# Attention output multiplied straight from PSUM, and four neighbours reordered, in a one-core decoder layer

## The chip, the cores and the metric

The kernel runs on one core of one Trainium2 chip. The metric is the device time of one execution in microseconds (us); a time is the median of several executions. The engines of the core are named as in the profile: PE (TensorE, matrix products and transposes), DVE (VectorE), ACT (ScalarE), POOL (GpSimd) and SP (SyncE, which issues nearly all DMAs here). Every engine works through its own list of instructions in order, and instructions on different engines wait for each other through semaphores.

## The reference, cut to what matters

One decoder layer on 32 batch elements of 256 tokens and 256 features, in float32: self attention with 16 heads of 64 (4 key and value heads, rotary positions, ALiBi bias), windowed cross attention with 16 heads of 16, and a feed-forward net with quantized weights and activations. Each part is followed by a residual and a layernorm.

```python
# self attention, the part that the change touches
q, k, v = x @ Wq, x @ Wk, x @ Wv          # 16 heads of 64; k and v of 4 heads
attn = q @ k.T / 8 + slopes * (key position - query position)
attn = softmax(attn)                      # over 256 keys
out  = (attn @ v) @ Wo
x = layernorm(x + out)
x = layernorm(x + cross_attention(x, ctx, cell))
x = layernorm(x + feed_forward(x))
```

## The kernel before, in words

**Tiling.** Tokens come in two tiles of 128 (`NT`), features in two chunks of 128 (`NDC`). Self attention of a batch element is cut into eight units (`self_units`, L383): two query tiles x two pairs of key heads x two halves of the heads that share them. A *pair* `m` is two units that share query tile and key heads; there are four pairs per batch element and 128 in all. Cross attention has four units per batch element.

**One self unit.** `self_scores` (L385) multiplies queries and keys into two PSUM banks `s`; DVE adds the ALiBi row and takes the minimum for the softmax in one instruction (L409). `self_exp` (L421) takes the exponential on ACT and sums it (L427). `self_turn` (L460) transposes the exponentials on PE into a bank `t` (L470) and ACT copies it out as `pT` (L475).

**One pair.** `self_values` (L477) multiplies `v` with four `pT` tiles into one bank `o` (L487); ACT copies the bank into the SBUF tile `oT` (L494). The softmax sums are turned separately: `self_inverse` (L436) takes the reciprocal on DVE (L441), DVE spreads it into the tile `wide` (L443), a transposing DMA on SP moves `wide` to `planes` (L448), and `self_spread` (L452) interleaves `planes` into `R` on POOL (L455). `wide`, `planes` and `R` have one buffer each. `self_normal` (L496) then multiplies `oT` by `R` on DVE (L500).

**Other work, cut into parts.** The projections (`self_inputs`, L330 to L354), the output projection and first layernorm (`self_output`, L502 to L555: the product `wo` L508, the factors `rs_x` on POOL L523 to L526, the normalized row `zq` on DVE L533, its transpose `zqT` copied out by ACT as `zT` L205, and the product `xq` L545), the cross attention's input (`cross_inputs`, with the factors `rstd_zc` L184 to L186 and the scaling of `cs` on ACT L198), its output and the feed-forward net (`feed_forward`: the products `ff` L811, tanh on ACT L825 and the products on DVE L826, the rounding steps L798 on POOL and L800 on DVE) are generators. At each `yield` a generator gives the number of slots until its next part.

**Order.** A loop written out by hand runs over slots, four to a pair (L905 to L953). In each slot it emits fixed steps of self attention and cross attention, and `parts()`, which emits the parts that are due. `flush()` at a slot's end emits what the parts have put off, such as the scaling of `cs`. For PE, DVE and ACT the order of emission is the order of execution (`manual_schedule`, L895). For POOL and SP a scheduler places the instructions, so a change in the emission order can move instructions on these two queues that the diff does not name. In slot 0 the two score units, four groups of exponentials, the values of pair `m - 1` and the cross attention's transposes come first; in slot 1 the parts, the cross attention's scores, values and half of its exponentials; in slot 2 the parts, the reciprocals and the transposes of the first unit; in slot 3 the transposes of the second unit, the parts and the spreading.

**Banks.** All PE outputs share one pool of eight PSUM banks (`bank`, L91). A bank that is read by ACT or DVE is free for a new product when that read has ended.

Of the kernel before, what the change touches and what calls it, by code (L numbers as in the profile page):

```python
# [14 lines left out]
ALU = mybir.AluOpType  # L15
# [36 lines left out]
def kernel(  # L52
# [27 lines left out]
    nc = tc.nc  # L80
# [5 lines left out]
    def ctile(shape, dtype, name):  # L86
        return const.tile(shape, dtype, name=name, tag=name)
# [3 lines left out]
    def bank(name, shape=(P, 512), dtype=F32):  # L91
        return ps.tile(list(shape), dtype, tag="b", name=name)
# [10 lines left out]
    def work(name, shape, bufs=2, dtype=F32):  # L103
        return sb.tile(list(shape), dtype, tag=name, name=name, bufs=bufs)
# [50 lines left out]
    for i in range(2):  # L155


        t = ctile([P, (NT + 1) * XH * XE + 32 - XE], F32, f"xvaug{i}")
# [33 lines left out]
    def flush():  # L192
        while last:
            last.pop(0)()
# [282 lines left out]
    def self_values(b, m):  # L477

        s = state[b]
        qc, kc, _rp = self_units[2 * m]  # L480
        pTs = [s.pop(("pT", 2 * m + rp)) for rp in range(2)]
        s["oT", qc, kc] = oT = work("oT", [P, NCH // 2, P], 3)
        po = bank("o")
        for kk in range(NT):
            for rp in range(2):
                for half in range(2):
                    nc.tensor.matmul(  # L487
                        po[half * HD : (half + 1) * HD, rp * L : (rp + 1) * L],
                        s["v"][:, kk, (2 * kc + half) * HD : (2 * kc + half + 1) * HD],
                        pTs[rp][half][:, kk * L : (kk + 1) * L],  # L490
                        start=(kk == 0 and rp == 0),
                        stop=(kk == NT - 1 and rp == 1),
                    )
        nc.scalar.copy(oT.rearrange("p c t -> p (c t)"), po)  # L494

    def self_normal(b, m):  # L496
        s = state[b]
        qc, kc, _rp = self_units[2 * m]
        oT = s["oT", qc, kc].rearrange("p c t -> p (c t)")
        nc.vector.tensor_tensor(oT, oT, s.pop(("R", m)), ALU.mult)  # L500

    def self_output(b, qc):  # L502

# [391 lines left out]
    with tc.manual_schedule(engines={mybir.EngineType.PE, mybir.EngineType.DVE, mybir.EngineType.Activation}):  # L895
        running = []
        slot = min(starts)
        while starts or running:
            m, part = divmod(slot, 4)
            k = m - CROSS  # L900
            for gen in starts.pop(slot, ()):
                running.append([slot, gen])

            def cross(f, unit, *more):
                if 0 <= unit < 4 * B:  # L905
                    f(*divmod(unit, 4), *more)

            def pair(f, unit):
                if 0 <= unit < 4 * B:
                    f(*divmod(unit, 4))  # L910

            def own(f, unit, *more):
                if 0 <= unit < 8 * B:
                    f(*divmod(unit, 8), *more)

            def parts():
                for r in list(running):
                    if r[0] == slot:
                        wait = next(r[1], r)
                        if wait is r:  # L920
                            running.remove(r)
                        else:
                            r[0] += wait or 1

            if part == 0:
                own(self_scores, 2 * m)
                own(self_scores, 2 * m + 1)
                own(self_exp, 2 * m, 0)
                own(self_exp, 2 * m, 1)
                own(self_exp, 2 * m + 1, 0)  # L930
                pair(self_values, m - 1)
                cross(cross_turn, k - 1, 0)
                cross(cross_turn, k - 1, 1)
                own(self_exp, 2 * m + 1, 1)
                parts()
                pair(self_normal, m - 1)
            elif part == 1:
                parts()
                cross(cross_scores, k)
                cross(cross_values, k - 1)  # L940
                cross(cross_exp, k, 0)
            elif part == 2:
                parts()
                pair(self_inverse, m)
                cross(cross_exp, k, 1)
                own(self_turn, 2 * m)
                cross(cross_back, k - 1)
            else:
                own(self_turn, 2 * m + 1)
                parts()  # L950
                pair(self_spread, m)
            flush()
            slot += 1  # L953
# [89 lines left out]
```

## Time and profile before

| what | us |
|---|---|
| median of 3 executions | 2209.63 (2208.27 to 2213.26) |
| the profiled execution, whole | 2211.08 |
| its span, first to last instruction | 2209.3 |
| PE busy | 2103.3 (95%) |
| DVE busy | 1789.9 (81%) |
| ACT busy | 1659.5 (75%) |
| POOL busy | 1316.8 (60%) |
| L494, ACT copy of `o` into `oT`, 128 times | 72.0 (563 ns each) |
| L500, DVE product `oT` x `R`, 128 times | 98.0 (765 ns each) |
| L455, POOL copy into `R`, 128 times | 173.5 (1356 ns each) |
| L443, DVE spreading of the reciprocals, 128 times | 108.2 (845 ns each) |

The busy times overlap, so they do not add up to the span. A group's idle time is the time that its engine stood still just before it, and its releaser is the instruction whose end let it go on. A timeline row gives the start and duration in us, the engine, the line, the operation, what it writes and reads, and in brackets the idle time before it with its releaser.

### The profile page before, as it was taken

The numbers are of one execution on the slowest core, as the hardware profiler recorded it, in microseconds if no ns is written. First come the engines' busy times: TensorE is split into PE (matmuls) and PEld (weight loads), VectorE is DVE, ScalarE is ACT, GpSimd is POOL, SyncE is SP. The second block draws the span as 40 slices with busy tenths as digits, with TensorE's granted clock in tenths as the row PEclk, the third lists the DMA queues.
The fourth block names the chain that finished last, engine by engine and source line by source line (L and its number), as shares of the span: only waits on it lengthen the run. The fifth ranks groups of instructions, "written<-read, shape, count | busy, mean of one in ns | idle before, by whom it ended". The sixth has DMA issues, their size and how long they took to land.

```text
span 2209.3 us, 54605 instructions
## 1 busy us (share of the span) xinstructions
PE 2103.3 (95%) x17254; PEld 1617.7 (73%) x17316; DVE 1789.9 (81%) x6949; ACT 1659.5 (75%) x4961; POOL 1316.8 (60%) x1977
## 2 busy tenths in 40 slices
PE   7899999999999999999999999999999999999984
PEld 5677777777777777777777777777777777777662
DVE  3877888888888888888888888888888888888775
ACT  2578778787778787778777778877777877777862
POOL 4465655666665666655656655656666556666542
PEclk8999999999999999999999999999999999999985
DMA  6433333333333334333333333334333333333221
GB/s 213 113 78 71 82 78 76 75 78 85 84 79 73 79 74 86 88 76 75 78 74 90 83 75 74 80 74 89 84 79 77 78 73 83 85 78 74 43 52 31
DMA packets 326592, 177.59 MB, mean 80 GB/s; under 512 B 242976, under 2 KB 296096, under 8 KB 326304
## 3 DMA queue, kind: packets, MB, share of 16 engines
q1 hardware_dynamic: 324608, 170.52, 34.1%
q10 hardware_dynamic: 1696, 3.57, 0.4%
q8 instruction: 138, 2.26, 0.4%
q14 instruction: 150, 1.23, 0.2%
HBM read 39.50 MB, written 8.39 MB: 22 GB/s over the span
## 4 chain that ended last, share of the span: by engine, by line
PE 58%; DVE 20%; ACT 12%; DMA 3%; issue 2%; POOL 1%; SPq 0%; ACTq 0%; POOLq 0%; DVEq 0%
PE wo L508 9%; PE t L470 8%; DVE p L409 7%; PE s L393 6%; ACT p L427 6%; PE o L487 5%; PE proj L330 5%; PE ff L811 4%; PE xq L545 3%; PE xt L708 3%; ACT xpT L710 3%; PE ffo L858 3%; PE xk L617 2%; PE xw L770 2%; PE v L362 2%; DMA out_dram<-x 2%
## 5 line engine op out<-in xcount | busy, mean ns | idle before, releaser
L427 ACT ACTIVATE p<-p,nm 128x256 f32<-128x256 f32 x1024 | 508.3, 499 | 235.8 <-DVE nm L409 235.8
L409 DVE CUSTOM_DVE_ANT_0 p<-s,alibi 128x256 f32<-128x256 f32 x1024 | 361.6, 416 | 3.2 <-PE s L393 3.2
L699 ACT ACTIVATE xp<-xp,xnm 128x128 f32<-128x128 f32 x1024 | 328.6, 401 | 47.0 <-DVE xnm L683 46.8
L393 PE MATMUL s<-kT,qT 64*128 64x256 f32 x2048 | 271.4, 392 | 0.0
L475 ACT COPY pT<-t 128x512 f32<-128x512 f32 x512 | 263.7, 598 | 7.0 <-PE t L470 6.8
L470 PE MATMUL t<-ident,p 128*128 128x128 f32 x2048 | 267.0, 273 | 0.9 <-ACT p L427 0.9
L354 POOL TENSOR_TENSOR qT<-qT,other 128x512 f32<-128x512 f32 x128 | 178.7, 1396 | 137.9 <-DMA other<-psin 113.1
L487 PE MATMUL o<-pT,v 128*64 128x256 f32 x2048 | 249.8, 386 | 0.0
L393 PEld LDWEIGHTS s<-kT,qT 64*128 64x128 f32 x2048 | 197.5, 187 | 68.6 <-issue 16.2
L330 PE MATMUL proj<-xT,wq_sb 128*128 128x256 f32 x1024 | 245.8, 384 | 0.0
L508 PE MATMUL wo<-wo_sb,oT 128*128 128x256 f32 x1024 | 244.1, 381 | 0.4 <-DVE oT L500 0.4
L470 PEld LDWEIGHTS t<-ident,p 128*128 128x128 f32 x2048 | 234.9, 142 | 9.4 <-ACT p L427 2.6
L683 DVE CUSTOM_DVE_ANT_0 xp<-xs,mask 128x128 f32<-128x128 f32 x1024 | 225.5, 284 | 13.2 <-PE xs L669 11.0
L508 PEld LDWEIGHTS wo<-wo_sb,oT 128*128 128x128 f32 x1024 | 192.9, 191 | 29.3 <-DVE oT L500 1.1
L487 PEld LDWEIGHTS o<-pT,v 128*64 128x64 f32 x2048 | 136.4, 137 | 98.1 <-issue 42.3
L330 PEld LDWEIGHTS proj<-xT,wq_sb 128*128 128x128 f32 x1024 | 187.7, 193 | 21.9 <-issue 0.4
L500 DVE TENSOR_TENSOR oT<-oT,R 128x512 f32<-128x512 f32 x128 | 98.0, 765 | 119.8 <-ACT oT L494 110.2
L427 ACT ACTIVATION_READ_ACCUMULATOR p<-p,nm 128x1 f32 x1024 | 194.1, 190 | 0.0
L455 POOL COPY R<-planes 128x1024 uint16<-128x1024 uint16 x128 | 173.5, 1356 | 21.9 <-DMA planes<-wide 21.6
L826 DVE SCALAR_TENSOR_TENSOR gu<-gu,ff 128x512 f32<-128x512 f32 x128 | 82.5, 684 | 100.7 <-ACT gu L825 100.6
L847 POOL TENSOR_SCALAR gu<-gu,ffhup 128x1024 f32<-128x1024 f32 x64 | 73.5, 1149 | 143.9 <-DVE ffhup L843 143.9
L708 PEld LDWEIGHTS xt<-ident,xp 128*128 128x128 f32 x1024 | 112.1, 143 | 49.0 <-issue 36.2
(147 smaller groups left out, 4530.8 us busy)
## 6 DMA issues: line engine op xcount, KB each, us to landing
other<-psin SPq DMA_DIRECT2D x640, 64.0 KB, 2.0
xT<-in_xt_dram SPq DMA_DIRECT2D x32, 256.0 KB, 2.8
xs<-in_x_dram SPq DMA_DIRECT2D x32, 256.0 KB, 2.7
cs<-in_ctx_dram SPq DMA_DIRECT2D x32, 256.0 KB, 2.8
other<-qb SPq DMA_DIRECT2D x64, 128.0 KB, 2.0
kTz<-tr SPq DMA_DIRECT2D x256, 32.0 KB, 2.0
other<-qb SPq DMA_DIRECT2D x128, 64.0 KB, 1.9
out_dram<-x SPq DMA_DIRECT2D x32, 256.0 KB, 2.4
```

Of the source, the lines that this page charges most:

```text
L330: nc.tensor.matmul(pq[:, c * L : (c + 1) * L], w[:, dc, c * P : (c + 1) * P], xT[:, dc, :], start=(dc == 0), stop=(dc == NDC - 1),)
L354: nc.gpsimd.tensor_tensor(d2, d2, other, ALU.add)
L393: nc.tensor.matmul(banks[half][:, rr * L : (rr + 1) * L], qT[rows_, rr, qc * P : (qc + 1) * P], kT[rows_, kc, :], start=(rr == 0), stop=(r ...
L409: nc.vector.tensor_tensor_reduce(p[:, cols], banks[half][:, cols], alibi[:, 2 * (4 * kc + 2 * rp + rr) + half, :], -0.125, 3.0e38, ALU.add ...
L427: nc.scalar.activation(p[:, cols], p[:, cols], AF.Exp, bias=nm[:, rr : rr + 1], scale=-1.0, accum_out=s["sums", i // 2][:, e : e + 1],)
L470: nc.tensor.transpose(pt[:, j * P : (j + 1) * P], p[half][:, rr * L + kk * P : rr * L + (kk + 1) * P], ident,)
L475: nc.scalar.copy(pT[half], pt)
L487: nc.tensor.matmul(po[half * HD : (half + 1) * HD, rp * L : (rp + 1) * L], s["v"][:, kk, (2 * kc + half) * HD : (2 * kc + half + 1) * HD], ...
L508: nc.tensor.matmul(py[:, 0:D], s["oT", qc, kc][:, r, :], wo_sb[:, 4 * kc + r, :], start=(kc == 0 and r == 0), stop=(kc == 1 and r == 3),)
L683: nc.vector.tensor_tensor_reduce(p[:, cols], banks[2 * half + j // 2][:, j % 2 * P : (j % 2 + 1) * P], s["mask"][:, qc, :], -1.0, 3.0e38, ...
L699: nc.scalar.activation(p[:, cols], p[:, cols], AF.Exp, bias=s["xnm", i][half][:, j : j + 1], scale=-1.0)
L708: nc.tensor.transpose(pt[:, j * P : (j + 1) * P], p[:, j * P : (j + 1) * P], ident)
```

## The change

The ACT copy of `o` into `oT` is taken out: `self_values` keeps the bank, and `self_normal` reads the bank on DVE and writes `oT`. In slot 0 `parts()` is emitted ahead of the last group of exponentials instead of behind it. In slot 2 `self_inverse` is emitted ahead of `parts()`. In slot 3 `parts()` is emitted ahead of the transposes of the second unit.

```diff
@@ self_values
-        nc.scalar.copy(oT.rearrange("p c t -> p (c t)"), po)
+        s["po", m] = po
@@ self_normal
-        nc.vector.tensor_tensor(oT, oT, s.pop(("R", m)), ALU.mult)
+        nc.vector.tensor_tensor(oT, s.pop(("po", m)), s.pop(("R", m)), ALU.mult)
@@ slot 0
                 cross(cross_turn, k - 1, 1)
+                parts()
                 own(self_exp, 2 * m + 1, 1)
-                parts()
                 pair(self_normal, m - 1)
@@ slot 2
+                pair(self_inverse, m)
                 parts()
-                pair(self_inverse, m)
                 cross(cross_exp, k, 1)
@@ slot 3
+                parts()
                 own(self_turn, 2 * m + 1)
-                parts()
                 pair(self_spread, m)
```

On POOL and SP the changed program stands in another order too. On SP the transposing DMA of `planes` moves forward. On POOL the copy into `R` (L455), which stood behind `rs_x` (L523 to L526) twice per batch element, stands ahead of it; once it stands ahead of `rstd_zc` (L184 to L186) and once ahead of L579 to L581. The first of the three products of the rotary step, L579, stands ahead of L798, where it stood behind.

## The prediction

> **What bounds the kernel now.** I read the table of stretches first, then the waits of TensorE (PE), then the timelines of all engines over one round. Between 70 us and 2140 us, at a granted clock of 1.00, PE is busy 2017.25 of 2070.00 us, and one wait holds most of the rest.
>
> ```profile
> 70.00:2140.00 2070.00, 2017.25 (x16775) 1558.55 (x16833) 1716.26 (x6733) 1617.47 (x4850) 1262.72 (x1882) 1.00 0.35 78
> ...
> PE xq L545 <- ACT zT L205: 37.8, 61, 0.8
> ```
>
> The work repeats once per batch element: the transpose `zqT` starts at 1058.03 and again at 1123.54, so a round is 65.51 us. In it PE waits twice at `xq`, 0.82 us (1062.40) and 0.43 us (1090.57), and PE's weight load once for 0.20 us at the scores after 1067.40 (releaser: the first `pT` copy). That is 1.45 us. The timelines, 1056 to 1124 us, show what stands around these waits:
>
> ```profile
> 1059.58 0.56 ACT L494 COPY oT<-o 128x512 f32<-128x512 f32 x1
> ...
> 1061.99 0.36 ACT L205 COPY zT<-zqT 128x256 f32<-128x256 f32 x1
> ...
> 1067.25 2.05 ACT L475 COPY pT<-t 128x512 f32<-128x512 f32 x4
> 1069.14 1.32 ACT L825 ACTIVATE gu<-ff,ffg 128x512 f32<-128x512 f32 x2
> ...
> 1081.65 0.72 POOL L525 TENSOR_TENSOR rs_x<-rs_x,neg_half 128x2 f32<-128x2 f32 x1
> ...
> 1086.30 1.35 POOL L455 COPY R<-planes 128x1024 uint16<-128x1024 uint16 x1 [1.17 <-DMA planes<-wide]
> ...
> 1098.22 0.70 POOL L184 TENSOR_SCALAR rstd_zc<-mv_zc 128x1 f32<-128x1 f32 x2
> ...
> 1100.53 1.09 ACT L198 ACTIVATE cs<-cs,rstd_zc 128x256 f32<-128x256 f32 x2 [2.36 <-POOL rstd_zc L186]
> ...
> 1104.94 1.06 ACT L710 COPY xpT<-xt 128x512 f32<-128x512 f32 x2
> ...
> 1116.31 1.36 POOL L798 TENSOR_SCALAR tr<-x,ffup 128x256 f32<-128x256 f32 x2
> ```
>
> Columns: start, duration, engine, line, operation, output and inputs. The reader is to see three things. From 1056.61 to 1070.46 ACT has no idle entry: it sets the pace there, and PE's waits only show it. On POOL (GpSimd) the copy that makes R, L455, stands behind the layernorm factors rs_x (L523 to L526). And ACT stands 2.36 us before 1100.53 for the factors rstd_zc.
>
> **The change part by part.** I read the order in which the changed kernel's instructions stand on each queue and the bank that each waits for; the durations are those above.
>
> **Copy removed (L494).** ACT loses 128 x 563 ns = 72 us, on PE's path 0.47 us per pass (1059.58 to 1060.04, where the next copy starts). VectorE (DVE) reads the bank. [...] the multiply from two SBUF tiles (L500) has a median of 693 ns and a mean of 765, the same shape with one PSUM operand (L339, L832) 684 and 682 median. I take the rows: nothing lost, 0 to 10 us of DVE time won, off the path. The bank `o` is now held until L500 ends; the fourth `xs` bank waits for that. L500 would end near 1088.7 and `xs` starts at 1088.85: cost 0, but with only 0.15 us to spare.
>
> **First slot.** The copy zT passes in front of two exponentials: with the oT copy gone, 0.47 + 0.98 us earlier. No DMA moves; in rounds with `xw` nothing else moves.
>
> **Third slot.** Reciprocal and spreading copy (L441, L443: 0.91 us, 1080.37 to 1081.28) go ahead of the slot's parts. Their transposing DMA moves forward on SP, in front of hiT and the `qb` and `xs` loads; those land 3 us or more before use, cost nothing. On POOL the R copy moves too, and passes waiting work: rs_x twice per round, rstd_zc once, and `qb`, `other`, `xqT` once. An R that waits for its DMA (3.1 us median to landing) now holds all these back.
>
> **Fourth slot.** PE's own work is the same. On ACT the two tanh (1.14 us) stand between the second and third `pT` copy; the product `o` needs the fourth. Elsewhere the copies have 1 us or more to spare.
>
> **The sum, in two stretches.** *From `xs` at 1075.31 to `wo` at 1105.93.* The last mask step (L683) ends 1077.73; reciprocal and spreading 0.91: 1078.65; DMA 3.1 and issue 0.05: 1081.8; R 1.35 and start: 1083.2; rs_x 1.28 (1114.68 to 1115.96): 1084.5; L533 0.76: 1085.3, where L409 starts (before: 1084.26). From there 0.51 to the first exponential, six of them 2.97, two xpT copies 0.96, zT 0.26: 1090.0. `xq` could start 1090.14 without its wait: the 0.43 goes, with nothing to spare. But DVE goes on late: eight L409 2.76, L500 0.62, L838 to L845 1.95, L339 and L346 1.2, eight L683 1.75, L441 and L443 0.95, L850 0.6, L838 to L843 1.82: 1096.95. Then POOL: gu 1.12, R 1.35, and rstd_zc until ACT can scale 2.31 (1098.22 to 1100.53): 1101.8, against 1100.53. ACT: scaling 0.99, six exponentials 2.97, first xpT copy 0.48: 1106.25. In the changed kernel `wo` takes the bank that this copy frees (before: one freed by DVE's L774). PE is there at 1105.50, waits 0.8 us, and starts at 1106.30. The stretch is 0.37 us longer, though its `xq` wait is gone.
>
> *From `xs` at 1107.76 to `o`.* L683 ends 1110.20; the same steps give R at 1115.6; rs_x to L526 1.65: 1117.3; L579, which now stands ahead of L798, 1.24: 1118.55; L798 twice 1.33: 1119.9. DVE's L800 needs it, was at 1119.59 and is now at 1119.95; L409 starts 0.37 us later (1122.0). The ACT chain behind it is 0.47 us shorter: its copies come 0.10 earlier. Counted one round back: second copy done 1068.1, two tanh 1069.25, third and fourth copy 1070.2. The third matmul of `o` starts at 1070.25; before, 0.49 us after 1069.81, at 1070.30. So the 0.82 us at `xq` and the 0.20 us at the scores are given back as waits at the scores and `o`: net -0.05 us.
>
> Per round +0.32 us. Two of the transposes stand bare on these paths, and their landing is not always 3.1 us (min/median/max 3.0/3.1/5.0); the rows of these two kinds average 0.2 us above, 13 of 64 at 3.6 to 5.0. Whether the long ones follow the moved DMA no row shows: between 0 and 0.44 us a round, I take 0.22. Sum: 0.54 us x 30 rounds = 16 us. Start and end (before 135 us, after 2107 us) I leave as they are, +-3 us. The profiled execution took 2211.08 us (span 2209.3); it becomes 2227. The median shown, 2209.63, lies 1.45 us below it: **2226 us**.
>
> **The rivals.** *All waits go (20 in 100).* The R copies come early enough to hold nobody back, and the `xq` waits vanish with nothing in their place: 2209.63 - 37.8 = 2172 us; with half of it won, 2191. For it: the waits are large and named, and L500's own waits for oT (110.2 us) go as well. Against it: rs_x today is done at 1082.37 (L525), and R cannot be done before 1083.2. It decides from R being done 1.2 us earlier than I put it in both stretches.
>
> *The two cancel (12 in 100).* My chain through rstd_zc is 0.4 us too long and the landings stay at 3.1: -0.05 us a round, 2208 us.
>
> *Landings get longer (8 in 100).* The transposes now run beside loads from which they were apart. At 3.7 us on average, two bare landings cost 1.2 us a round instead of 0.22: 30 x 0.98 = 29 us more, 2255 us. For it: 5.0 is in the rows. Against it: the median is 3.1 in every position.
>
> **How the numbers follow.** My forecast has 60 in 100; its own range is 2212 to 2245, from the landings' two ends (10 to 23 us) and 0.3 us a round for the two chains. The change is not to be told from none within 0.2%, that is 2205.2 to 2214.0. Faster: the first rival, 0.20. Same: the second and the low edge of mine, 0.13. Slower: the rest, 0.67. The range leaves out the better part of the first rival and the upper end of the last: 2190 to 2256.
>
> **What would show it.** Right: `xq` waits for zT nearly gone; new PE waits at `wo` (releaser ACT's xpT) near 0.8 us a round, and at the scores or `o` (releaser ACT's pT or DVE's L826) near 1 us; L455 ahead of L523 with the DMA as its releaser, and L533 waiting for rs_x; the ACT wait before the cs scaling above 2.36 us; L500 near 684 ns. Wrong: if PE's idle time in the stretch from 70 to 2140 us falls below 40 us, or L533 does not wait for L525. If L500 takes over 750 ns, the row was the wrong one.

## The result, and the profile after

The changed kernel takes 2237.72 us (median of 4, 2236.22 to 2238.36), the kernel before 2211.18 (median of 4, 2208.27 to 2213.26) beside it: a ratio of 1.012, with a 95% interval of 1.0103 to 1.0138. It is 26.5 us slower. The direction was forecast, and 2237.72 lies in the range; the size was forecast at 16 us.

**Where the time is.** The span grows by 27.3 us, from 2209.3 to 2236.6. Taken at DVE's reduction L785, of which there is one per batch element: the first starts 4.9 us later (196.5 against 191.6), the 31 rounds between the first and the last take 22.3 us more (2008.4 against 1986.1), and what follows the last takes 0.1 us more. The loss is therefore a small one in every round, 0.72 us, plus 4.9 us at the start.

The table of stretches of the changed kernel, with the same columns as before (length, then busy time and count of PE, weight load, DVE, ACT and POOL, then the granted clock):

```profile
70.00:2140.00 2070.00, 2023.96 (x16686) 1558.88 (x16685) 1701.90 (x6669) 1549.13 (x4682) 1213.21 (x1865) 1.00 0.34 78
```

This row is easily misread. PE's idle time falls from 52.75 to 46.04 us in the same 2070 us, although every round is longer. About half of the fall is not real: the trace before lacks 62 matmul records of `ff` (L811), and the gaps in front of `ff`, which the changed trace does not have, count as 3.3 us of idle time there. The rest does not mean that PE lost less time. The records of a group's matmuls overlap (in `o` each takes 0.38 to 0.43 us, and two start every 0.22 us), so a short wait in the middle of a group lengthens the group instead of showing as idle time of PE. The waits name what the row hides (columns: who waited for whom, us in total, times, longest us):

```profile
ACT cs L198 <- POOL rstd_zc L186: 118.7, 31, 4.8
...
DVE row L533 <- POOL rs_x L525: 51.1, 30, 3.3
...
DVE xib L800 <- POOL tr L798: 22.5, 30, 1.7
...
PE wo L508 <- ACT xpT L710: 14.4, 28, 1.4
...
PE t L470 <- DVE gu L826: 12.6, 29, 0.4
```

`xq` no longer waits for zT on PE. In its place, once a round each, stand PE's waits at `wo` and at the second `t`, and two new waits of DVE for POOL. Before, these two were:

```profile
DVE row L533 <- POOL rs_x L525: 1.1, 1, 1.1
...
DVE xib L800 <- POOL tr L798: 0.5, 1, 0.5
```

The chain of waits says the same in one row, first before the change, then after it. The longest way through the program ran over PE first and now runs over DVE first:

```profile
PE 58%; DVE 20%; ACT 12%; DMA 3%; issue 2%; POOL 1%; SPq 0%; ACTq 0%; POOLq 0%; DVEq 0%
```

```profile
DVE 35%; PE 30%; ACT 14%; POOL 9%; issue 6%; DMA 5%; SPq 0%; DVEq 0%; POOLq 0%; ACTq 0%
```

**The stretch to `wo`,** in the timeline of the changed kernel (start, duration, engine, line, operation, and in brackets the idle time before with its releaser):

```profile
1161.78 1.34 POOL L455 COPY R<-planes 128x1024 uint16<-128x1024 uint16 x1 [5.09 <-DVE gu L832]
1163.21 0.22 POOL L523 TENSOR_SCALAR rs_x<-mv_x 128x1 f32<-128x1 f32 x1
...
1164.52 0.41 DVE L533 TENSOR_SCALAR row<-row,mv_x,rs_x 128x256 f32<-128x256 f32 x1 [1.65 <-POOL rs_x L525]
...
1177.53 1.34 POOL L455 COPY R<-planes 128x1024 uint16<-128x1024 uint16 x1
1178.96 0.70 POOL L184 TENSOR_SCALAR rstd_zc<-mv_zc 128x1 f32<-128x1 f32 x2
...
1181.11 1.09 ACT L198 ACTIVATE cs<-cs,rstd_zc 128x256 f32<-128x256 f32 x2 [3.67 <-POOL rstd_zc L186]
...
1185.06 1.04 ACT L710 COPY xpT<-xt 128x512 f32<-128x512 f32 x2
1185.68 1.99 PE L508 MATMUL wo<-wo_sb,oT 128*128 128x256 f32 x8 [0.23 <-ACT xpT L710]
```

POOL stands idle for 5.09 us in front of R. The named releaser, L832, has nothing to do with R: `wide` is written at 1158.50, and the transposing DMA takes 3.1 us, which makes 1161.6. So it was the DMA that let R go. Behind R waits rs_x, behind rs_x DVE's L533; and 16 us later a second R stands ahead of rstd_zc, whose lateness reaches `wo` through ACT.

**The stretch to `o`,** same kernel and view, one round in two places:

```profile
1133.40 1.28 POOL L580 TENSOR_TENSOR other<-other,rx_sb 128x512 f32<-128x512 f32 x1
1133.48 1.49 DVE L800 TENSOR_SCALAR xib<-tr 128x512 bf16<-128x512 f32 x1 [0.72 <-POOL tr L798]
...
1145.73 1.09 PE L470 MATMUL t<-ident,p 128*128 128x128 f32 x8 [0.44 <-DVE gu L826]
...
1146.84 1.07 ACT L475 COPY pT<-t 128x512 f32<-128x512 f32 x2
1147.78 1.30 ACT L825 ACTIVATE gu<-ff,ffg 128x512 f32<-128x512 f32 x2
...
1148.93 1.11 ACT L475 COPY pT<-t 128x512 f32<-128x512 f32 x2
1149.28 2.33 PE L487 MATMUL o<-pT,v 128*64 128x256 f32 x16 [0.18 <-DVE gu L826]
...
1150.09 1.05 PEld L487 LDWEIGHTS o<-pT,v 128*64 128x64 f32 x10 [0.19 <-ACT pT L475]
```

Here are the two tanh between the `pT` copies. The product `o` takes 2.33 us instead of 1.95: 0.38 us of waiting inside a group, which PE's row does not show as idle. The last row, of PE's weight loads, names what the group waited for: the last `pT` copy, which ends at 1150.04. L800, which took 0.95 us as a rule before, takes 1.49.

For comparisons of whole rounds I set all rounds of a kernel at the start of `xk` (L617) and took the median start of each step over 23 rounds. Against before, the changed kernel's first `xq` comes 0.67 us earlier, `xt` behind `o` 0.46 us later, the second `xq` at the same time, `wo` 0.65 us later and the next round 0.74 us later.

### The profile page after: what moved, and what is told of

The parts are those of the page before. It is cut to its first block, busy times and chain, and to the rows that moved or that the text cites. A ratio compares the mean times of both kernels' runs of the same rounds, so it can differ in the third digit from the quotient of the medians.

```text
span 2236.6 us, 54579 instructions
## 1 busy us (share of the span) xinstructions
PE 2133.7 (95%) x17316; PEld 1632.2 (73%) x17316; DVE 1790.9 (80%) x6949; ACT 1606.0 (72%) x4833; POOL 1277.2 (57%) x1977
## 4 chain that ended last, share of the span: by engine, by line
DVE 35%; PE 30%; ACT 14%; POOL 9%; issue 6%; DMA 5%; SPq 0%; DVEq 0%; POOLq 0%; ACTq 0%
PE wo L508 8%; DVE p L409 7%; ACT p L427 4%; PE o L487 4%; DVE xp L683 4%; ACT xp L699 3%; DVE ffm L838 3%; ACT gu L825 2%; PE xk L617 2%; DVE st L177 2%; PE xs L669 2%; DVE hib L850 2%; DMA planes<-wide 2%; DVE xib L800 2%; ACT xpT L710 2%
## 5 line engine op out<-in xcount | busy, mean ns | idle before, releaser
L475 ACT COPY pT<-t 128x512 f32<-128x512 f32 x512 | 274.9, 595 | 141.7 <-PE t L470 140.2
L409 DVE CUSTOM_DVE_ANT_0 p<-s,alibi 128x256 f32<-128x256 f32 x1024 | 361.8, 416 | 8.9 <-PE s L393 8.9
L470 PE MATMUL t<-ident,p 128*128 128x128 f32 x2048 | 269.3, 274 | 13.5 <-DVE gu L826 12.6
L455 POOL COPY R<-planes 128x1024 uint16<-128x1024 uint16 x128 | 171.4, 1339 | 193.5 <-DVE gu L832 123.2
L487 PE MATMUL o<-pT,v 128*64 128x256 f32 x2048 | 261.6, 386 | 6.9 <-DVE gu L826 5.2
L508 PE MATMUL wo<-wo_sb,oT 128*128 128x256 f32 x1024 | 248.1, 386 | 14.4 <-ACT xpT L710 14.4
L354 POOL TENSOR_TENSOR qT<-qT,other 128x512 f32<-128x512 f32 x128 | 165.2, 1291 | 135.2 <-DMA other<-psin 101.5
L508 PEld LDWEIGHTS wo<-wo_sb,oT 128*128 128x128 f32 x1024 | 193.6, 192 | 50.2 <-ACT xpT L710 21.0
L487 PEld LDWEIGHTS o<-pT,v 128*64 128x64 f32 x2048 | 144.6, 136 | 110.3 <-issue 31.0
L826 DVE SCALAR_TENSOR_TENSOR gu<-gu,ff 128x512 f32<-128x512 f32 x128 | 82.4, 683 | 112.0 <-ACT gu L825 112.0
L607 POOL TENSOR_SCALAR mask<-ck_i,cq_sb 64x128 f32<-64x128 f32 (+1 forms) x96 | 86.1, 897 | 102.7 <-DVE xnm L683 96.7
L708 PE MATMUL xt<-ident,xp 128*128 128x128 f32 x1024 | 142.0, 281 | 0.7 <-ACT xp L699 0.7
```

The source lines that it names most:

```text
L409: nc.vector.tensor_tensor_reduce(p[:, cols], banks[half][:, cols], alibi[:, 2 * (4 * kc + 2 * rp + rr) + half, :], -0.125, 3.0e38, ALU.add ...
L455: nc.gpsimd.tensor_copy(R.bitcast(U16).rearrange("p (n z) -> p z n", z=2), s.pop(("planes", m)).rearrange("p z r q -> p z (r q)"),)
L470: nc.tensor.transpose(pt[:, j * P : (j + 1) * P], p[half][:, rr * L + kk * P : rr * L + (kk + 1) * P], ident,)
L475: nc.scalar.copy(pT[half], pt)
L487: nc.tensor.matmul(po[half * HD : (half + 1) * HD, rp * L : (rp + 1) * L], s["v"][:, kk, (2 * kc + half) * HD : (2 * kc + half + 1) * HD], ...
L508: nc.tensor.matmul(py[:, 0:D], s["oT", qc, kc][:, r, :], wo_sb[:, 4 * kc + r, :], start=(kc == 0 and r == 0), stop=(kc == 1 and r == 3),)
```

## The experiments

**Which edit carries the loss.** Four kernels were run together; the kernel before took 2211.14 us beside them.

The changed kernel without its third-slot edit:

```diff
-                pair(self_inverse, m)
                 parts()
+                pair(self_inverse, m)
```

> The changed kernel with the third slot's edit undone: the reciprocals stand behind the parts again, and on POOL the copy R stands behind rs_x and rstd_zc as before. Theory 1 (the loss comes from R ahead of rs_x and rstd_zc on POOL, and a smaller part from the fourth slot's transposes behind the tanh): L533 no longer waits for rs_x, the 118.7 us before the cs scaling fall back to about 84, no PE wait at wo; 37.8 us at xq stay won, 0.3 to 0.5 us a round stay lost at the fourth slot: 2185 to 2200 us. Rival (the loss comes from the bank o held until L500, or from longer landings of the transposing DMA): no or little gain, 2228 us or more.

Measured: 2185.15 us, ratio 0.9879 (0.9865 to 0.9894). L533's wait for rs_x is back at 1.1 us, the wait before the cs scaling is 62.8 us, and PE waits 0.2 us in all at `wo` for xpT. The third slot's edit costs 52.6 us in this company; the rival falls.

The changed kernel without its fourth-slot edit:

```diff
-                parts()
                 own(self_turn, 2 * m + 1)
+                parts()
```

> The changed kernel with the fourth slot's edit undone: the second unit's transposes stand ahead of the parts again. POOL's order stays that of the changed kernel. Theory 1: the waits of t and o for L826 go (17.8 us on PE), the wait at wo (14.4 us) stays: 2215 to 2228 us, L533 still waits for rs_x in 30 rounds. Rival (the fourth slot alone makes the loss): the wait at wo goes as well and the time is 2180 us or less.

Measured: 2225.10 us, 1.0063 (1.0046 to 1.008). The fourth slot's edit costs 12.6 us here. (POOL's order is not quite that of the changed kernel: once a round L535, the addition of `xbias`, stands ahead of the factors rstd_zo again, so its place is part of the 12.6 us.) The waits of `t` and `o` for L826 are gone (a wait of `ff` of 11.9 us for it appears), `wo` still waits 12.2 us, L533 35.1.

The first two edits alone:

```diff
-        nc.scalar.copy(oT.rearrange("p c t -> p (c t)"), po)
+        s["po", m] = po
...
+                parts()
                 own(self_exp, 2 * m + 1, 1)
-                parts()
```

> The first two edits alone: oT multiplied from the bank, and the first slot's parts ahead of the last exponentials; POOL's order is that of the kernel before. Theory 1: the waits of 37.8 us at xq and 5 us at the scores go, and nothing takes their place: 2172 to 2182 us. Rival (the bank o, held until L500, is the cost): PE waits for L500 at xs or elsewhere, 2205 us or more.

Measured: 2181.10 us, 0.9863 (0.9848 to 0.9878). The bank held until L500 costs nothing that shows. Of the two `xq` waits only the second is truly won: the first `xq` comes 1.26 us earlier, but the `o` behind it only 0.09, since ACT's `pT` copies are late in its place.

The third slot's edit alone:

```diff
+                pair(self_inverse, m)
                 parts()
-                pair(self_inverse, m)
```

> The third slot's edit alone on the kernel before: reciprocals ahead of the parts, oT still copied by ACT. Theory 1: R ahead of rs_x makes L533 late by about 1 us in two stretches of a round, the xq waits grow: 2235 to 2265 us. Rival (order on POOL costs nothing; landings or the bank make the loss): 2205 to 2215 us.

Measured: 2304.47 us, 1.0419 (1.0402 to 1.0437). The sign is right, the size is not: 93 us instead of 24 to 54. It is not L533's wait here (1.6 us in all): on POOL R stands ahead of rs_x only once a round in this kernel. L798 starts 3.79 us later in its round, L800 waits 42.5 us for it and DVE's L409 comes 2.06 us later; ACT, which still has the copy of oT, passes it on to PE. Of the 3.02 us that a round loses, 1.2 us come only at its end, between the fourth `xs` and the product behind it (L724); ACT's wait before the cs scaling is 149.8 us here against 84.1 before, but what makes this part was not shown. In the company of the first two edits the same edit costs 44 us (2225.10 against 2181.10).

**Is it R's place on POOL?** The edit moves three things: DVE's reciprocals, a DMA on SP, and R on POOL. To part them, all four edits stay and R is held back on POOL. `issue_after` queues R behind given instructions of POOL:

```diff
+        with ExitStack() as behind:
+            for name in ("rs_x", "zc", "q"):
+                if name in factors:
+                    behind.enter_context(tc.issue_after(factors[name].ins))
+            nc.gpsimd.tensor_copy(
...
-        nc.gpsimd.tensor_scalar(rs[:, 2:3], mv[:, 0:1], rs[:, 0:1], -1.0, ALU.mult, ALU.mult)
+        factors["rs_x"] = nc.gpsimd.tensor_scalar(rs[:, 2:3], mv[:, 0:1], rs[:, 0:1], -1.0, ALU.mult, ALU.mult)
```

`factors["zc"]` and `factors["q"]` hold L186 and L798 in the same way. In these kernels the line numbers behind L455 are 8 higher, so DVE's L533 is L541, L508 is L516, L710 is L718 and L800 is L808; POOL's rs_x, L525, is L533 there.

> The changed kernel with all four edits, and the copy R held back on POOL alone: it is queued behind the factors rs_x and rstd_zc and the rounding step L798, as it stood before the change. The reciprocals stay ahead of the parts on DVE, their transposing DMA stays forward on SP. Theory 1 (the third slot's edit costs 44 to 53 us through R's place on POOL): L533's 51.1 us of waits for rs_x and L800's 22.5 us go, the wait at wo goes: 2184 to 2198 us. Rival (it costs through the 0.91 us of DVE work ahead of the parts, or through the DMA's place on SP): 2220 us or more.

Measured: 2169.30 us, 0.981 (0.9796 to 0.9825). The queues of DVE, ACT and SP have the order of the changed kernel, so the 68.4 us between the two are lost on POOL, and DVE's and SP's part of the edit costs nothing. R stands idle for 22.6 us in all, and 22.3 of these end with its transposing DMA. The time is below what the theory gave, since the edit in this form gains (2169.30 us against 2185.15 without it).

On POOL, R is not the only one that moved: the scheduler put L579 behind L798 again, moved L535 behind rstd_zo once more a round, and mixed the two halves of rstd_zc. The 68.4 us are R's place with what moved along. In the changed kernel R (1.34 us) and L579 (1.28 us) both stand ahead of L798; no run here has one of them there without the other.

The first row of its chain of waits:

```profile
PE 81%; ACT 7%; DVE 6%; issue 3%; DMA 2%; POOL 1%; SPq 0%; ACTq 0%; POOLq 0%; DVEq 0%
```

PE has the chain again, and a round is 1.28 us shorter than before the change.

**Which of the things behind R?** The list in the loop above is cut to one name each, in the order `("rs_x",)`, `("zc",)`, `("q",)`; the kernel before took 2211.69 us beside these and the last run. L579 goes back behind L798 in the first and the third of them and stays ahead of it in the second.

> The changed kernel, R held back on POOL behind rs_x alone; it stays ahead of rstd_zc and of L798. If the wait of L533 for rs_x carries the loss: at most a third of the 68 us between the changed kernel and the one with R held back behind all three stays, 2170 to 2192 us, and the wait at wo is under 0.5 us a round. Rival (rstd_zc and the scaling of cs carry it): 2205 us or more, with the wait at wo still 0.8 us a round.

Measured: 2175.99 us, 0.9839 (0.9822 to 0.9855). PE waits only 1.4 us in all at `wo`, although R still stands ahead of rstd_zc and ACT still waits 89.4 us before the cs scaling:

```profile
PE wo L516 <- ACT xpT L718: 1.4, 3, 0.8
```

> The changed kernel, R held back on POOL behind rstd_zc alone; it stays ahead of rs_x twice a round and of L798. If the wait of L533 for rs_x carries the loss: 2215 to 2235 us, L533 waits about 50 us as in the changed kernel. Rival (rstd_zc carries it): 2175 to 2200 us, no wait at wo.

Measured: 2217.19 us, 1.0024 (1.0016 to 1.0033).

```profile
DVE row L541 <- POOL rs_x L533: 51.3, 31, 3.0
...
DVE xib L808 <- POOL tr L806: 23.1, 30, 1.8
...
PE wo L516 <- ACT xpT L718: 1.3, 3, 0.5
```

DVE's two waits for POOL are those of the changed kernel, but of the wait at `wo` only 1.3 us are left. The two runs together show how that wait is made: DVE must be late by L533, *and* a second R must stand ahead of rstd_zc. Either alone leaves next to none of it. (The halves of rstd_zc are mixed in the second of these runs. The first half is ready about 1.5 us sooner behind `gu` there, and R's own 1.34 us are most of that.)

> The changed kernel, R held back behind L798, which takes it behind the first rs_x of a round too; in the other stretch R stays ahead of rs_x and of rstd_zc. The stretch from the cross scores to o should be mended (1.2 us a round in the trace of the kernel with R held back in both), the one to wo not (0.8 us a round): 2187 to 2205 us, L533 waiting in one of its two places a round. Rival (one stretch carries all): 2170 us or 2235 us.

Measured: 2201.18 us, 0.9953 (0.9938 to 0.9968).

```profile
PE wo L516 <- ACT xpT L718: 14.4, 28, 1.3
...
DVE row L541 <- POOL rs_x L533: 51.4, 31, 3.0
```

The stretch to `o` is mended, the one to `wo` is as in the changed kernel. So L533's 51 us all lie in the stretch to `wo`. In the stretch to `o` the loss goes through L798, which stands behind R and L579, and through L800. The mended stretch gives 36.5 us.

**The first, second and fourth edit alone.** The kernel before took 2211.06 us beside these. The copy's removal, the first half of the diff above for the first two edits:

> The first edit alone: oT multiplied from the bank, all orders of emission as before. The zT copy comes 0.47 us earlier: the 0.43 us at the second xq go, 0.47 of the 0.82 us at the first go. Theory 1: 2185 to 2198 us, and L500 near 684 ns. Rival (the DVE multiply from the bank is dearer, or the held bank stalls PE): 2205 us or more.

Measured: 2182.44 us, 0.9868 (0.9854 to 0.9883). Nearly all that the first two edits bring together.

The first slot's order alone, the second half of that diff:

> The second edit alone: the first slot's parts ahead of the last exponentials, oT still copied by ACT. The zT copy comes 0.98 us earlier, so both xq waits go (1.25 us a round), but ACT has as much work as before up to the pT copies, and PE waits for these instead: of the 0.82 us nothing stays, of the 0.43 us all: 2196 to 2204 us. Rival (both gains stay): 2172 to 2180 us.

Measured: 2202.49 us, 0.9963 (0.995 to 0.9975). The expectation held: `xq` 0.80 us earlier, `o` 0.10 later, the second `xq` 0.38 earlier.

The fourth slot's order alone:

```diff
+                parts()
                 own(self_turn, 2 * m + 1)
-                parts()
```

> The fourth slot's edit alone on the kernel before. Theory 1: it costs 0.1 to 0.5 us a round, as the second transposes wait for the bank that L826 frees and the product o for the later pT copies: 2213 to 2226 us. Rival (it costs only behind a late DVE, as in the changed kernel): 2208 to 2213 us.

Measured: 2204.20 us, 0.9968 (0.9955 to 0.9981). Both expectations miss: it gains 6.9 us. The stretch to `o` does lose 0.27 us a round. But the second L533 of a round takes 0.38 us where it took 0.82: that is 0.44 us a round won, and the net of 0.2 us a round is the gain measured. What differs around the instruction is shown in the last section.

**A kernel that beats both.** R held back behind all three, and the fourth slot as it was before:

> R held back behind all three, and the fourth slot's edit undone. If the fourth slot's edit costs also when DVE is early (tanh ahead of two pT copies): 2155 to 2166 us, faster than the 2169.3 with it. Rival (it gains, as it did alone on the kernel before): 2173 to 2190 us, with PE waiting at the scores or at o for ACT's pT.

Measured: 2145.66 us, 0.9704 (0.9689 to 0.9718), 66 us below the kernel before and 92 below the changed one, and below the range that was expected. The 23.6 us to the kernel with the fourth slot's edit are not all that edit's: in POOL's order L535 moved at two places a round, and L800 and L533 are shorter as well (below). The run cannot part the two.

## Why the prediction was right, and where its sum was off

- **Copy removed.** Held. The row was the right one: L500 has a median of 678 and a mean of 671 ns (98.0 us became 85.9). On DVE it is 12.1 us less, where 0 to 10 were put. The edit alone gains 28.6 us, so the held bank cost nothing that shows. In the changed kernel, where DVE is late, the weight loads of `xs` do wait for L500, 9.8 us in 31 rounds; the product behind `xs` (L724) waits for ACT's xpT there.
- **First slot.** Held; zT is early, and the waits at `xq` are gone from PE's list.
- **Third slot, the stretch to `wo`.** Held in mechanism, somewhat too large in size. Forecast 0.37 us a round, measured 0.65 - 0.46 = 0.19 at `wo` and 0.28 at the next round's start; PE waits 0.51 us a round at `wo` where 0.8 was put. The chain as put was: rs_x behind R, DVE late, R ahead of rstd_zc, xpT's bank late for `wo`. The runs with R behind rs_x alone and behind rstd_zc alone show that both places of R are needed, and the row of `wo` names xpT. One term was 0.35 us too long: L533 was taken at 0.76 us and takes 0.41.
- **Fourth slot, the stretch to `o`.** The step that failed in size. It was put as "net -0.05 us" and measured +0.46, an error of 0.51 us a round. About two thirds of it are one term: L800 was moved by its wait alone ("L409 starts 0.37 us later"). It starts 0.14 us later and takes 1.48 us instead of 0.95, so L409 starts 0.68 us later, and with it ACT's copies: the first `pT` 0.23 us late where 0.10 early was put, the third about 1.3 us late where about 1.0 was put. The sum treats POOL as a queue and leaves out that L800 got longer beside POOL's work. The wait of the second `t` for the bank that L826 frees (12.6 us in all) was not in the sum, and does not make `o` late: from its first exponential behind L409 to the last `pT` copy ACT has no idle time in any of 28 rounds (13.35 us), and in the round shown above the rest of `o` starts 0.05 us behind that copy. ACT's chain sets `o`; the wait of `t` lies beside it.
- **Landings.** Nothing of it: the transposes took 3.27 us on average against 3.35 before, and the two kinds that the sum counts 3.21 against 3.32, so the 0.22 us a round have to be struck. By luck this term covered almost half of the former error.
- **Start and end.** Put at +-3 us; the start cost 4.9, the end 0.1. What the 4.9 are made of stays open.
- **The sum.** The direction was right, and the stretch to `wo` gave its part as forecast. But of the 0.74 us that a round loses, 0.46 come from the stretch to `o`, which was put at nothing, and none from the landings; so 16 us were put where 26.5 came. With the measured terms: 30 x 0.74 + 4.9 = 27 us.
- **The rivals.** "All waits go" had the right price: 2172 us was put, and the kernel with R held back takes 2169.3. It fell on the condition named, R's being done too late on POOL. "The two cancel" fell with the clear loss. "Landings get longer" fell by 3.27 against 3.35. The expectation that PE's idle time would not fall under 40 us held with 46.0 but was a poor test: the kernel at 2185 us has 35.5, the one at 2304 us has 80.2, and the changed kernel, in between, hides its waits inside groups.

## What to carry to other kernels

When emission order is changed and only some queues are held by hand, compare the order on the scheduler's queues as well: here one copy that moved ahead of two rows of layernorm factors on an engine busy 57% of the time cost 68 us, together with what moved along with it. That is more than the 30 us that the first two edits were worth. A small result that others wait for should stand ahead of a bulky copy that waits for a DMA, whichever would be "ready" first by plan. And a wait in the middle of a matmul group need not show as idle time of PE (0.38 us in `o` here): compare the length of a group and the start of the next step, round against round.

## What the runs showed of the hardware

Two DVE instructions, L800 and L533, took two to three and a half times as long when a POOL instruction that had started first was still at work 0.15 us after their start. In the changed kernel L800 took 1.32 to 1.49 us in the 30 such cases and 0.43 us in the two others; L533 has a median of 0.81 us in 32 such cases and 0.41 us in the 32 others. The durations (min/median/max ns) of L800, before the change, in the changed kernel and in the best one (there L808), each from the view of one line:

```profile
L800 DVE TENSOR_SCALAR xib<-tr x32: 427/948/1573, 196.7 to 2180.1; 128x512 bf16<-128x512 f32 x32
```

```profile
L800 DVE TENSOR_SCALAR xib<-tr x32: 426/1484/1489, 200.7 to 2207.3; 128x512 bf16<-128x512 f32 x32
```

```profile
L808 DVE TENSOR_SCALAR xib<-tr x32: 415/418/1152, 200.5 to 2117.0; 128x512 bf16<-128x512 f32 x32
```

The same instruction on the same shape has a median of 948, 1484 or 418 ns; what stands on POOL around it differs. Its end followed the end of the POOL instruction. In the rows of the stretch to `o` above, L580 ends at 1134.68 and L800 at 1134.97. In all 30 of those cases of the changed kernel L800 ended 0.28 us after it, and in the 28 cases before the change likewise. In one round of the best kernel POOL's L587 ends at 1093.43 and L808 at 1093.71, 0.28 us after it too, and L808 takes 0.93 us there; its short time, 0.42 us, is the median. L533 is alike, with about 0.15 us instead of 0.28 (60 cases before, 32 in the changed kernel): a median of 816 ns before, 382 in the best kernel. In the kernel with the first two edits alone, L800 and L533 take 0.95 and 0.82 us in the stretch to `o`, in the best one 0.42 and 0.38; L800 starts at the same place of the round in both, and L409 0.96 us earlier in the best one. That is the sum of the two differences, and it is where the best kernel's lead over that one begins.

Which of the two was the longer one changed with hundredths of a microsecond. One round of the kernel before and one of the kernel with the fourth slot's order alone, in the timeline (POOL has L535 at the same place in its order in both):

```profile
1083.46 0.72 POOL L535 TENSOR_TENSOR x<-x,xbias 128x256 f32<-128x256 f32 x1 [0.72 <-ACT x L534]
...
1083.50 0.83 DVE L533 TENSOR_SCALAR row<-row,mv_x,rs_x 128x256 f32<-128x256 f32 x1
```

```profile
1081.07 0.38 DVE L533 TENSOR_SCALAR row<-row,mv_x,rs_x 128x256 f32<-128x256 f32 x1
...
1081.17 0.87 POOL L535 TENSOR_TENSOR x<-x,xbias 128x256 f32<-128x256 f32 x1 [0.72 <-ACT x L534]
```

POOL's L535 starts 0.04 us ahead of L533 in the first and 0.10 us behind it in the second, and the later one is the longer one. Before the change all 28 full rounds are alike: L535 starts 0.04 to 0.06 us ahead, and L533 takes 0.82 to 0.84 us. With the fourth slot's order alone the median of L533 over all its 64 times is 414 ns, against 816 before. This is the 0.44 us a round that made the fourth slot's edit a gain when it stood alone.

The multiply L500 shows the other side. With two SBUF inputs it took 0.69 us in the 72 cases without a POOL instruction beside it and 0.86 on average (at most 1.76) in the 56 with one; from the bank, in the changed kernel, it takes 0.66 without and 0.67 with one. Why an instruction takes longer beside one of another engine, and why L500 does not when it reads the bank, was not shown by any run.
